# Two graph layers in one pass: layer 1's sums and blocks, q's writes, the flag and three loads put into other steps

## The chip, the core and the metric

The kernel runs on one core of a Trainium2 chip. The core has five engines that run their own instruction streams and wait for one another by semaphores: TensorE (PE in the profile; PEld is its weight load), VectorE (DVE), ScalarE (ACT), GpSimd (POOL) and SyncE (SP), which here only issues DMAs. Each engine runs its instructions in the order of the program, so one that waits holds back everything behind it on its engine; this is true of the DMAs that SP and POOL issue, too. The metric is the time of one execution on the device in microseconds.

## The reference, cut to what matters

Sixteen graphs of 1024 nodes with 256 features pass through two layers. Each layer normalises the nodes, applies relu and adds its result to its input.

```python
# layer 0: masked attention, 8 heads of 32 features
h = relu(layernorm(x))
Q, K, V = proj(h, Wq, bq), proj(h, Wk, bk), proj(h, Wv, bv)
scores = where(adj == 0, -inf, Q @ K.T * HD ** -0.5)
x = x + (softmax(scores) @ V) @ Wo.T + bo

# layer 1: attention by the kind of edge; each kind k has a vector a_k
h = relu(layernorm(x))
e_k = leaky_relu((h * a_k) @ h.T, 0.2)
scores = e_0 where adj == 1, e_1 where adj == 2, e_2 where adj == 3, e_3 where adj == 4, else -9e15
x = x + softmax(scores) @ h
```

In the inputs adj holds only 0 and 1. The kernel's main pass computes layer 1 with a_0 alone; a flag for each tile of adj records whether other kinds occur, and a second pass behind the main one, which these inputs skip, does such graphs again.

## The kernel before, in words

The unit of work is a tile of 128 rows (query nodes) of one graph; there are 16 x 8 = 128 of them. The program's order is written out by hand under `tc.manual_schedule()`: a loop over s = 0 to 136 (L720), called a round here, and in it a loop over the steps h = 0 to 7 (L723), one for each head. With b, t = divmod(s, 8), t = 0 is a graph's first round. In round s several tiles are at different stages:

- `now` is the tile of layer 0 whose heads are scored: per step two score matmuls of 512 columns (L415) into one of two PSUM tiles, the masked maximum on VectorE (L427), and a step later the exponential on ACT (L435). `was` is the tile of the round before and `gone` that of two rounds before; `nxt` is the tile that comes.
- `piece` and `piece_was` are a tile of nodes eight to nine rounds ahead of its use: normalised, turned, projected to k, v and q. The k and q halves are written to DRAM (L295, L301) and loaded again as keys (L336, on POOL, in steps of the last and first round of a graph) and queries (L382, on SP, step 1).
- `edge` is the tile of layer 1 scored in this round, nine rounds behind layer 0; `edge_was` is that of the round before, whose sums are made in this one.

The probabilities have to be turned before they are multiplied with the values. Heads 1, 3, 5, 7 are turned by eight TensorE transposes (L527) and two ACT copies (L528), two steps after their scores. Heads 0, 2, 4, 6 (`BY_BLOCKS`) and layer 1's tile are turned by VectorE within blocks of 32 (L356, `turn_blocks`) and moved to their places by four DMAs of 128 KB on SP's queue (L361, `placed`, called by `place_blocks`). Heads 0 to 5 are turned in steps 2 to 7 of their own round, heads 6 and 7 in steps 0 and 1 of the next. The sums over heads 0 to 3 (`combine(0)`, L470, 32 small matmuls, which are 64 rows of the trace; over key tiles, and within one over the four heads) come in step 7, those over heads 4 to 7 (`combine(1)`) in step 3 of the next round. Behind them in step 4 come the query projections of `piece_was` (L257), which write the bank `early` out of which VectorE takes v (`biased`, L331) at the start of that step, and the output projection (L485), for which VectorE makes oT (L480). In step 5 VectorE makes the layer's result x1 with its statistics (`residual`), POOL follows with some 18 small instructions that give scale and shift (`norm_of`, L143), and ACT normalises in step 7 (L506); TensorE transposes that at the end of step 0 (L513) and ACT copies it into layer 1's key table h1T (L517).

Layer 1's tile is scored in steps 0 and 1 (L549), its maximum and its leak are taken in steps 2 and 3 (L563, L571), its exponential in step 4 (L575), and its blocks are turned in step 5. Its sums (`gather`, L593) and `store` (L602, L603) come a round later. Its places, the tile pT1, exist once; so do adj, x1b, sel and ha. The mask of a tile (`mask`, L397, POOL) is kept for ten tiles, since layer 1 uses it again; `flag` (L406, ACT) squares adj less one half and sums the row.

On SP, one ordinary round issues, from step 0: k's first half (1), head 6 of `was` (4), k's second half (1), the next queries (1), head 0 (4), head 2 (4), q's two halves (2, step 6), head 4 (4, step 6), x1d (1), out (1, step 7), layer 1's blocks (4, step 7).

Of the kernel before, what the change touches and what calls it, by code (L numbers as in the profile page):

```python
# [42 lines left out]
def gnn_kernel(  # L43
# [131 lines left out]
    class Piece:  # L175
# [5 lines left out]
        def __init__(self, b, first, n=1):  # L181
            self.b, self.first, self.n = b, first, n
            self.cols = slice(first * P, (first + n) * P)
            self.projected, self.halved, self.again = [], [], []
            self.tags = ("xin", "h0", "hT", "halves", "hTm") if n == 1 else ("pT", "pT", "qt", "p", "blocks")

        def buffer(self, i, shape, dtype=F32):
# [88 lines left out]
        def split(self):  # L276
            which, oc, ps, bias, halves, parts = self.halved.pop(0)
            nc.vector.scalar_tensor_tensor(  # L278
                parts[:, 1], ps, bias[:, oc : oc + 1], parts[:, 0].bitcast(F32), ALU.add, ALU.subtract
            )  # L280
            halves = halves.bitcast(F32)
            if which == 0:
                self.write_keys(oc, halves, nc.sync, 0)
                if self.n > 1:
                    self.write_keys(oc, halves, nc.scalar, 1)
                self.again.append((oc, halves))
            elif self.n > 1:
                to = qds[self.b][self.first : self.first + self.n, oc]
                for twice in range(2):
                    (nc.sync, nc.scalar)[twice].dma_start(  # L290
                        out=to[:, :, twice].rearrange("t p w n -> p t (w n)"),
                        in_=halves.rearrange("p (t x) -> p t x", t=self.n),
                    )
            else:
                nc.sync.dma_start(  # L295
                    out=qds[self.b][self.first, oc].rearrange("p u w n -> p u (w n)"),
                    in_=halves.unsqueeze(1).to_broadcast([P, 2, 2 * P]),
                )
# [71 lines left out]
    class Attend:  # L370
# [21 lines left out]
            nc.gpsimd.dma_start(out=self.xb, in_=mixed(x[self.b, self.rows, :]))  # L392

        def mask(self):
            self.neg = work.tile([P, N], BF16, tag="neg", bufs=KEPT)
            masks[self.b, self.t] = self.neg
            nc.gpsimd.tensor_scalar(self.neg, self.adj, 0.0, MASKED, ALU.is_equal, ALU.mult)  # L397
            self.sums = small.tile([P, HEADS], F32, tag="sums")

# [2 lines left out]

        def flag(self):

            i = self.b * NT + self.t
            nc.scalar.activation(  # L406
                self.adj.bitcast(F32), self.adj, AF.Square, bias=less_half,
                accum_out=kinds_seen[:, i : i + 1],
            )

        def scores(self, h):
# [271 lines left out]
    with tc.manual_schedule():  # L683
# [8 lines left out]
        now, piece_next = attend_of(0), piece_of(0)  # L692
        nxt = attend_of(1)
        now.load()
        now.mask()
        now.flag()
        nxt.load()
        piece_next.load()
        for piece in first:
# [20 lines left out]
        for s in range(B * NT + LAG + 1):  # L720
            b, t = divmod(s, NT)
            nxt2, edge_nxt, piece_nxt = attend_of(s + 2), edges_of(s + 1), piece_of(s + 1)
            for h in range(HEADS):  # L723
                ending, eh = (now, h - 1) if h >= 1 else (was, HEADS - 1)
                turning, th = (now, h - 2) if h >= 2 else (was, HEADS + h - 2)


                if now:
                    now.scores(h)
                if h == 0 and piece_was:  # L730
                    piece_was.split()
                if h == 1 and piece_was:
                    piece_was.split()
                if h == 2 and edge:
                    edge.softmax_max()
                if h == 3 and edge:
                    edge.leak()
                if h == 4 and piece_was:
                    piece_was.biased()
                if h == 4 and was:  # L740
                    was.combined()
                if h == 5 and was:
                    was.residual()
                if h == 6 and piece_was:
                    piece_was.split()
                    piece_was.split()
                if h == 7 and edge_was:
                    edge_was.store()
                if now:
                    now.softmax_max(h)  # L750


                if ending:
                    ending.softmax_exp(eh)


                if turning and th in BY_BLOCKS:
                    turning.turn_blocks(th)
                    turning.place_blocks(th)
                elif turning:  # L760
                    turning.turn(th, 0)
                    turning.turn(th, 1)


                if h == 0:
                    if piece_was:
                        piece_was.write_again()
                    if edge:
                        edge.score(0)
                    if gone:  # L770
                        gone.turn_normed()
                        gone.turned_normed()
                    if nxt and s:
                        nxt.load()
                    if edge_was:
                        edge_was.load_nodes()
                if h == 1:
                    if edge:
                        edge.score(1)
                    if was:  # L780
                        was.reciprocals()
                    if piece:
                        piece.stats()
                        piece.scaled()
                    if piece_was:
                        piece_was.write_again()
                    if nxt:
                        nxt.load_queries()
                if h == 2:
                    if piece_was:  # L790
                        piece_was.values()
                    if was:
                        was.turn_reciprocals()
                        was.turned_reciprocals()
                        was.add_bias()
                if h == 3:
                    if was:
                        was.combine(1)
                    if nxt:
                        nxt.mask()  # L800
                if h == 4:
                    if piece_was:
                        piece_was.project(1, 0)
                        piece_was.project(1, 1)
                    if was:
                        was.output()
                    if piece:
                        piece.normed()
                    if edge:
                        edge.softmax_exp()  # L810
                    if edge_nxt:
                        edge_nxt.prepare()
                if h == 5:
                    if piece:
                        piece.turn()
                    if edge_was:
                        edge_was.gather(0)
                    if piece_was:
                        piece_was.high()
                        piece_was.high()  # L820
                    if piece:
                        piece.turned()
                    if piece_nxt:
                        piece_nxt.load()
                    if edge:
                        edge.turn_blocks()
                if h == 6:
                    if edge_was:
                        edge_was.gather(1)
                    if was:  # L830
                        was.keep()
                    if now:
                        now.load_nodes()
                    if nxt:
                        nxt.flag()
                    if piece:
                        piece.project(0, 0)
                        piece.project(0, 1)
                if h == 7:
                    if now:  # L840
                        now.combine(0)
                    if edge:
                        edge.place_blocks()
                    if piece:
                        piece.high()
                        piece.high()
                    if was:
                        was.normed()
                if now and t == NT - 1 and b + 1 < B and h in KEY_STEPS:
                    load_key(b + 1, KEY_STEPS.index(h))  # L850
                if now and t == 0 and b > 0 and HEADS + h in KEY_STEPS:
                    load_key(b, KEY_STEPS.index(HEADS + h))
            gone, was, now, nxt = was, now, nxt, nxt2
            edge_was, edge = edge, edge_nxt
            piece_was, piece = piece, piece_nxt
# [52 lines left out]
```

## Time and profile before

| | us |
|---|---|
| five runs, median | 3498.61 |
| lowest and highest of them | 3485.57 to 3503.91 |
| the profiled execution's own time | 3488.9 |
| its span, first to last instruction | 3487.1 |
| TensorE, VectorE, ACT, POOL busy in it | 3134.0, 2782.6, 2436.9, 2281.7 |
| mean granted TensorE clock | 0.969 of full speed |

The page of the profile gives busy time by engine, groups of instructions by line of the program with the idle time of their engine before them and what ended it ("<-"), and DMAs with the median time from issue to landing: 3.9 us for the blocks (2560 issues), 6.3 us for adj, 4.6 us for the queries, 5.8 us for the keys. A "wait" is idle time of an engine that another engine's instruction, or a DMA, ended; waits of an engine that is not the bottleneck cost nothing by themselves. In a timeline each row has its start, its length, the engine, the line, the operation and how many of them were merged ("x4"), and in brackets the idle time before it. SPq is SP's queue of instructions, and the length of a row there is that of issuing, not of moving the data.

### The profile page before, as it was taken

How to read it: one execution, taken by the hardware profiler on the slowest of the kernel's cores; microseconds unless marked ns; L12 is line 12 of the kernel's file. 1: busy time of each engine (PE TensorE's matmuls, PEld its weight loads, DVE VectorE, ACT ScalarE, POOL GpSimd, SP SyncE). 2: the span in 40 equal slices, each digit the busy share in tenths (PEclk: the TensorE clock that was granted, in tenths of full speed). 3: DMA queues.
4: the chain of work that ended last, by engine and by line, in shares of the span. 5: the costliest groups of instructions: out<-in, count | busy, mean ns of one | idle time of the engine just before them, and what ended most of it. 6: DMA issues, size and time to landing. Idle time of an engine off the chain costs nothing. (4 is left out here: it accounts for less than half of the span.)

```text
span 3487.1 us, 100532 instructions
## 1 busy us (share of the span) xinstructions
PE 3134.0 (90%) x36018; PEld 2278.1 (65%) x36018; DVE 2782.6 (80%) x5111; ACT 2436.9 (70%) x4829; POOL 2281.7 (65%) x6008
## 2 busy tenths in 40 slices
PE   5778999999999999999999999999999999998997
PEld 3666666666666666666676666666666666666653
DVE  3778878788788888888888788888878888887863
ACT  2777767677677777777777777777767777776750
POOL 2677667667667676667767767667667766765431
PEclk8999999999999999999999999999999999999999
DMA  5777787877778687786777778677787877777642
GB/s 211 207 220 225 211 250 209 246 220 222 229 224 247 202 240 226 209 256 206 246 221 219 244 216 244 204 229 235 207 248 217 248 212 213 243 219 231 189 131 76
DMA packets 747594, 763.10 MB, mean 219 GB/s; under 512 B 71792, under 2 KB 692592, under 8 KB 747088
## 3 DMA queue, kind: packets, MB, share of 16 engines
q1 hardware_dynamic: 678800, 542.21, 51.9%
q0 software_dynamic: 65088, 210.16, 20.0%
q8 instruction: 291, 4.77, 0.6%
q10 hardware_dynamic: 3200, 4.19, 0.3%
q14 instruction: 215, 1.76, 0.1%
HBM read 252.98 MB, written 167.77 MB: 121 GB/s over the span
## 5 line engine op out<-in xcount | busy, mean ns | idle before, releaser
L435 ACT ACTIVATE p<-p,nmx 128x1024 f32<-128x1024 f32 x1024 | 1185.9, 1158 | 414.4 <-DVE nmx L427 407.9
L427 DVE CUSTOM_DVE_ANT_0 p<-s,neg 128x1024 f32<-128x1024 f32 x1024 | 1243.0, 1214 | 205.2 <-PE s L415 204.2
L415 PE MATMUL s<-k,qt 128*128 128x512 f32 x2048 | 800.2, 472 | 34.5 <-DVE nmx L427 17.9
L470 PE MATMUL acc<-pT,v 128*32 128x128 f32 x16384 | 600.5, 289 | 238.5 <-DMA pT<-blocks 234.0
L470 PEld LDWEIGHTS acc<-pT,v 128*32 128x32 f32 x16384 | 494.6, 116 | 314.3 <-issue 216.6
L528 ACT COPY pT<-trp 128x512 f32<-128x512 f32 x1024 | 544.8, 584 | 132.2 <-PE trp L527 127.5
L356 DVE STREAM_TRANSPOSE blocks<-p 128x1024 f32<-128x1024 f32 x512 | 635.1, 1240 | 0.8 <-issue 0.8
L527 PE MATMUL trp<-ident,p 128*128 128x128 f32 x4096 | 533.3, 273 | 0.0
L527 PEld LDWEIGHTS trp<-ident,p 128*128 128x128 f32 x4096 | 481.6, 141 | 69.9 <-issue 1.2
L593 PE MATMUL acc<-h,pT 128*32 128x256 f32 x8192 | 510.8, 384 | 9.0 <-DMA pT<-blocks 8.2
L549 PE MATMUL s<-h1T,ha 128*128 128x512 f32 x1024 | 481.3, 593 | 0.5 <-ACT h1T L517 0.5
L397 POOL TENSOR_SCALAR neg<-adj 128x1024 bf16<-128x1024 int32 x128 | 467.7, 3654 | 18.6 <-DVE top L563 6.8
L415 PEld LDWEIGHTS s<-k,qt 128*128 128x128 f32 x2048 | 332.0, 193 | 217.9 <-issue 135.0
L593 PEld LDWEIGHTS acc<-h,pT 128*32 128x32 f32 x8192 | 246.7, 110 | 225.3 <-issue 79.7
L160 POOL TENSOR_SCALAR sq<-sq 128x1 f32<-128x1 f32 (+1 forms) x750 | 266.5, 355 | 65.5
L454 POOL COPY wide<-rec 128x256 f32<-128x256 f32 x128 | 51.2, 400 | 383.6 <-DVE rec L452 383.6
L301 POOL DMA_DIRECT2D kd<-halves x240 | 174.6, 727 | 165.6 <-DVE halves L278 148.7
L549 PEld LDWEIGHTS s<-h1T,ha 128*128 128x128 f32 x1024 | 183.9, 190 | 141.2 <-issue 128.7
L563 DVE CUSTOM_DVE_ANT_0 sel<-s,neg 128x1024 f32<-128x1024 f32 x128 | 156.7, 1224 | 70.9 <-PE s L549 70.9
L435 ACT ACTIVATION_READ_ACCUMULATOR p<-p,nmx 128x1 f32 x1024 | 202.6, 198 | 0.0
L517 ACT COPY h1T<-acc 128x256 f32<-128x256 f32 x128 | 47.7, 372 | 210.4 <-PE acc L513 210.4
L575 ACT ACTIVATE sel<-sel,nmx 128x1024 f32<-128x1024 f32 x128 | 145.3, 1135 | 64.5 <-DVE sel L571 64.5
(106 smaller groups left out, 4379.5 us busy)
## 6 DMA issues: line engine op xcount, KB each, us to landing
pT<-blocks SPq DMA_DIRECT2D x2560, 128.0 KB, 3.9
qt<-qd SPq DMA_DIRECT2D x128, 512.0 KB, 4.6
adj<-in_adj POOLq DMA_DIRECT2D x127, 512.0 KB, 6.3
qd<-halves SPq DMA_DIRECT2D x240, 256.0 KB, 2.6
k<-kd POOLq DMA_DIRECT2D x120, 512.0 KB, 5.8
kd<-halves SPq DMA_DIRECT2D x240, 128.0 KB, 4.2
kd<-halves POOLq DMA_DIRECT2D x240, 128.0 KB, 3.8
xb<-in_x POOLq DMA_DIRECT2D x128, 128.0 KB, 3.6
```

What stands on the lines that cost most here:

```text
L160: g.tensor_scalar(sq, sq, 1.5, None, ALU.add)
L301: queue.dma_start(out=kds[self.b][oc, :, :, twice, self.cols], in_=halves.rearrange("p (w n) -> p w n", w=2),)
L356: nc.vector.transpose(blocks.rearrange("p b j q -> p j b q"), p)
L397: nc.gpsimd.tensor_scalar(self.neg, self.adj, 0.0, MASKED, ALU.is_equal, ALU.mult)
L415: nc.tensor.matmul(self.ps[:, cols], lhsT=self.qt[:, h, :], rhs=keysets[self.b][h][:, cols], start=True, stop=True,)
L427: nc.vector.tensor_tensor_reduce(out=p, in0=sides[h in (3, 5, 7)], in1=self.neg, scale=-SCALE, scalar=FLOOR, op0=ALU.add, op1=ALU.min, acc ...
L435: nc.scalar.activation(p, p, AF.Exp, bias=nmx, scale=-1.0, accum_out=self.sums[:, h : h + 1])
L470: nc.tensor.matmul(sums_place[r * HD : (r + 1) * HD, g * P : (g + 1) * P], lhsT=vs[self.b][:, j, place_of(h) : place_of(h) + HD], rhs=self ...
L527: nc.tensor.transpose(tr[:, j, :], p[:, jj * P : (jj + 1) * P], ident)
L528: copy(pT[:, half * 4 : half * 4 + 4, :], tr)
L549: nc.tensor.matmul(self.e[:, cols], lhsT=self.ha[:, c, :], rhs=h1Ts[self.b][:, c, cols], start=(c == 0), stop=(c == NC - 1),)
L593: nc.tensor.matmul(sums_place[a * HD : (a + 1) * HD, :], lhsT=self.pT[:, j, a], rhs=h1s[self.b][:, j, :], start=(j == 0), stop=(j == NT - 1),)
```

## The change

The same instructions are issued, in other places:

- `gather(0)` and `gather(1)` of layer 1 go from steps 5 and 6 to steps 4 and 5, the first behind the output projection, the second behind the turn of `piece`.
- layer 1's `place_blocks` goes from step 7 to step 5, right behind its `turn_blocks`, and so ahead of head 4's blocks (step 6) on SP.
- q's two halves are no longer written to DRAM at the end of `split` (step 6, ahead of head 4's blocks) but by a new `write_queries` in step 7, behind `out`.
- `flag` goes from step 6 to step 3, ahead of `mask`, and writes its square into `neg`, which the mask then overwrites, in place of into adj itself. So the mask on POOL waits for ACT.
- adj is loaded in step 4 of the round before, behind the mask that reads the tile last, in place of step 0.
- layer 1's x1 is loaded in step 2 in place of step 0, on POOL, between `add_bias` and the mask.
- `turned_normed` (L517) goes from the end of step 0 to step 1, behind ACT's exponential of head 0.

The diff, cut to its core:

```diff
             else:
+                self.queries.append((oc, halves))
+
+        def write_queries(self):
+            for oc, halves in self.queries:
                 nc.sync.dma_start(
                     out=qds[self.b][self.first, oc].rearrange("p u w n -> p u (w n)"),
                     in_=halves.unsqueeze(1).to_broadcast([P, 2, 2 * P]),
...
         def mask(self):
+            nc.gpsimd.tensor_scalar(self.neg, self.adj, 0.0, MASKED, ALU.is_equal, ALU.mult)
+            self.sums = small.tile([P, HEADS], F32, tag="sums")
...
+        def flag(self):
...
+            i = self.b * NT + self.t
             self.neg = work.tile([P, N], BF16, tag="neg", bufs=KEPT)
             masks[self.b, self.t] = self.neg
...
             nc.scalar.activation(
-                self.adj.bitcast(F32), self.adj, AF.Square, bias=less_half,
-                accum_out=kinds_seen[:, i : i + 1],
+                self.neg, self.adj, AF.Square, bias=less_half, accum_out=kinds_seen[:, i : i + 1]
             )
...
                     ending.softmax_exp(eh)
 
+                if h == 1 and gone:
+                    gone.turned_normed()
...
                     if gone:
                         gone.turn_normed()
-                        gone.turned_normed()
-                    if nxt and s:
-                        nxt.load()
-                    if edge_was:
-                        edge_was.load_nodes()
                 if h == 1:
...
                         was.add_bias()
+                    if edge_was:
+                        edge_was.load_nodes()
                 if h == 3:
                     if was:
                         was.combine(1)
                     if nxt:
+                        nxt.flag()
                         nxt.mask()
                 if h == 4:
...
                         was.output()
+                    if edge_was:
+                        edge_was.gather(0)
...
                         edge_nxt.prepare()
+                    if nxt2:
+                        nxt2.load()
                 if h == 5:
                     if piece:
                         piece.turn()
                     if edge_was:
-                        edge_was.gather(0)
+                        edge_was.gather(1)
...
                         edge.turn_blocks()
+                        edge.place_blocks()
                 if h == 6:
-                    if edge_was:
-                        edge_was.gather(1)
                     if was:
                         was.keep()
                     if now:
                         now.load_nodes()
-                    if nxt:
-                        nxt.flag()
...
                 if h == 7:
                     if now:
                         now.combine(0)
-                    if edge:
-                        edge.place_blocks()
+                    if piece_was:
+                        piece_was.write_queries()
                     if piece:
                         piece.high()
                         piece.high()
```

More of the change, by code (lines that the diff above doesn't have):

```diff
@@ L183, in __init__ @@
             self.cols = slice(first * P, (first + n) * P)
-            self.projected, self.halved, self.again = [], [], []
+            self.projected, self.halved, self.again, self.queries = [], [], [], []
             self.tags = ("xin", "h0", "hT", "halves", "hTm") if n == 1 else ("pT", "pT", "qt", "p", "blocks")
@@ L394, in mask @@
         def mask(self):
-            self.neg = work.tile([P, N], BF16, tag="neg", bufs=KEPT)
-            masks[self.b, self.t] = self.neg
             nc.gpsimd.tensor_scalar(self.neg, self.adj, 0.0, MASKED, ALU.is_equal, ALU.mult)
@@ L405, in flag @@
             i = self.b * NT + self.t
+            self.neg = work.tile([P, N], BF16, tag="neg", bufs=KEPT)
+            masks[self.b, self.t] = self.neg
             nc.scalar.activation(
-                self.adj.bitcast(F32), self.adj, AF.Square, bias=less_half,
-                accum_out=kinds_seen[:, i : i + 1],
+                self.neg, self.adj, AF.Square, bias=less_half, accum_out=kinds_seen[:, i : i + 1]
             )
@@ L694, in gnn_kernel @@
         now.load()
+        now.flag()
         now.mask()
-        now.flag()
         nxt.load()
```

## The prediction, made before the changed kernel ran

> **What bounds the kernel now.** I read the shares by engine first, then the list of waits, then the timelines of one round (one pass of the loop over s, eight steps h) engine by engine. S is the start of a round's first score matmul; times "S + x" are us after it.
>
> ```profile
> PE 3134.0 (90%) x36018; PEld 2278.1 (65%) x36018; DVE 2782.6 (80%) x5111; ACT 2436.9 (70%) x4829; POOL 2281.7 (65%) x6008
> L470 PE MATMUL acc<-pT,v 128*32 128x128 f32 x16384 | 600.5, 289 | 238.5 <-DMA pT<-blocks 234.0
> ```
>
> TensorE is busy 90%, and of its 353 us of idle time 234 stand before one line: L470, the sums of layer 0, waiting for the DMAs that place a transposed head (pT<-blocks).
>
> ```profile
> PE acc L470 <- DMA pT<-blocks: 234.0, 122, 5.4
> ACT h1T L517 <- PE acc L513: 210.4, 122, 2.4
> POOL wide L454 <- DVE rec L452: 383.6, 127, 6.0
> DVE oT L480 <- PE acc L470: 103.3, 75, 5.6
> ```
>
> 122 waits in 128 rounds: one a round. L470 runs twice a round, combine(0) in step 7 and combine(1) in step 3; sorted by place, 233 us belong to combine(1), and its first four rows run (two matmuls, heads 4 and 5), so the missing tile is the next one: head 6, turned in step 0. One round (S = 1560.47), first the queue of SP:
>
> ```profile
> 1561.09 0.60 SPq L603 DMA_DIRECT2D out<-ot  x1
> 1561.79 3.67 SPq L361 DMA_DIRECT2D pT<-blocks  x4
> 1565.56 0.57 SPq L301 DMA_DIRECT2D kd<-halves  x1
> 1566.23 2.51 SPq L361 DMA_DIRECT2D pT<-blocks  x4
> ```
>
> ```profile
> 1562.51 1.24 DVE L356 STREAM_TRANSPOSE blocks<-p 128x1024 f32<-128x1024 f32 x1
> ...
> 1570.99 1.21 DVE L427 CUSTOM_DVE_ANT_0 p<-s,neg 128x1024 f32<-128x1024 f32 x1
> ...
> 1572.14 0.42 DVE L331 TENSOR_TENSOR v<-acc,bv_t 128x256 f32<-128x256 f32 x1
> ```
>
> ```profile
> 1569.06 0.41 PE L470 MATMUL acc<-pT,v 128*32 128x128 f32 x4
> 1571.05 1.94 PE L470 MATMUL acc<-pT,v 128*32 128x128 f32 x60 [1.58 <-DMA pT<-blocks]
> 1572.92 0.74 PE L415 MATMUL s<-k,qt 128*128 128x512 f32 x2
> 1573.50 1.05 PE L257 MATMUL acc<-hTm,wqT 128*128 128x128 f32 x8
> ```
>
> VectorE has head 6 turned at 1563.75, but SP issues its four DMAs only from 1566.23: the four of layer 1's tile (1561.79) and k's write stand ahead. Over rounds 17 to 117, for t = 1 to 7: head 6 is turned at S + 3.28, its DMAs are issued from S + 4.54, the last at S + 7.22, and TensorE resumes at S + 10.63, 3.41 us later; it was ready at S + 8.59. At t = 0, the first round of a graph: last issue S + 8.42, resume S + 14.35, ready S + 9.59.
>
> **What the bubble hides.** VectorE's last maximum before the sums ends at S + 11.74 in every ordinary round (11.72 at the least), then comes v (0.42 us), to S + 12.1. The query projections (L257, hTm) overwrite the bank that v reads, so they cannot start before about S + 12.15. They start at S + 13.36 on average for t = 1 to 7 and at S + 18.49 for t = 0; from there to the next S it is 12.2 us in both (periods 25.52 and 30.77). So of a 1.6 us bubble only 13.36 - 12.15 = 1.21 us can come back; the rest becomes a wait of L257 for v.
>
> **The parts.**
>
> *Layer 1's blocks issued in step 5 instead of step 7, its gathers a step earlier.* From the turn of head 4 to the last DMA of head 6, SP issues 4 + x1d + out + 4 + k + 4 = 15 now and, with q's two writes come in, 4 + x1d + out + 2 + k + 4 = 13 after. One costs 0.60 to 0.65 us. But the gathers (1.87 us each, the spacing from 1576.90 to 1578.77) now stand before the scores of heads 5 and 6, so these move back: laying the same durations end to end from L257 at S + 12.15 (0.89 projections, 0.68 output, 1.87 gather, 0.65 scores, 0.87 turn, 0.31 piece, 1.87 gather) puts the scores of head 6 at S + 19.3, and VectorE turns head 4 by S + 22.4, 1.9 us before the next S (S + 24.3) instead of 3.5 (now 1555.76 + 1.24, before 1560.47). The last issue for head 6 is then 12 issues of 0.65 after that: S + 5.95 if nothing holds the queue, 7.2 at worst (as now). With the 3.41 us from issue to resume: 9.4 to 10.6. A resume up to S + 9.55 costs nothing (1.9 for the sums, 0.6 for the scores, to 12.15). The added wait is on SP: the blocks of step 5 overwrite the tile that gather(1) reads, so they go out when it ends, S + 19.3 to 21.9; behind them stand only head 4's, not turned before S + 22.4. gather(0) overwrites the sums that oT is made from, but the output ahead of it waits for oT already. I take a projection start of S + 12.4: 0.96 us a round, between 0.2 and 1.21. Rounds with layer 1's tiles and t > 0: 105, so 101 us.
>
> *t = 0.* There head 6's DMAs take 5.93 us to resume, among key loads, adj (512 KB) and x1 (128 KB) issued in step 0; adj and x1 go elsewhere. Against it, the keys of heads 2 and 3 are issued on POOL after a chain that gets 1.4 us longer (below), and scores already wait there (L415 <- DMA k<-kd, 11.1 us in all). I take projections at S + 14.5, bounds 13.4 and 17: 4.0 us, 14 rounds, 56 us.
>
> *flag before mask* (ACT to step 3; POOL's mask now waits for it).
>
> ```profile
> 1570.05 1.05 ACT L528 COPY pT<-trp 128x512 f32<-128x512 f32 x2
> 1572.31 1.15 ACT L435 ACTIVATE p<-p,nmx 128x1024 f32<-128x1024 f32 x1 [1.21 <-DVE nmx L427]
> ```
>
> ```profile
> 1573.60 3.65 POOL L397 TENSOR_SCALAR neg<-adj 128x1024 bf16<-128x1024 int32 x1
> ...
> 1583.16 0.22 POOL L164 TENSOR_SCALAR shift<-shift 128x1 f32<-128x1 f32 x1
> ```
>
> ACT sits idle 1.21 us where the flag goes (1.17 + 0.2 us), so the next exponential slips by 0.2 us and ACT, busy 70%, absorbs it. The flag ends near S + 12.0; the mask starts at S + 11.7 on average now, and 0.68 us later with x1's load ahead of it. Wait: 0, at most 0.3 us. Writing bf16 in place of f32: nothing to gain or lose beyond a tenth of the 1.17 us, off the path.
>
> *x1 and adj loads* on POOL, 0.68 us each, go from step 0, where POOL idles 3.0 us a round for `wide` (383.6 / 127), into its dense stretch ahead of the normalisation: the last shift ends at S + 24.7 instead of 23.3. ACT is ready for it at S + 24.0, and head 7's exponential behind it (1.35 us) is needed by the turn at next S + 2.98; that leaves about 0.9 us unused. Cost 0, or up to 0.3 us a round with keys in the queue (t = 7). Both transfers are needed half a round or more later.
>
> *h1T's copy a step later on ACT* takes away 210 us of ACT idle, off the path; head 0's exponential comes earlier and nobody waits for it. 0. *q's writes in step 7* are counted in SP's 13; their readers come seven rounds on. The nine last rounds (layer 1 alone, 9.5 us each) issue the blocks before `out`: 0.5 us each, 5 us.
>
> **Sum:** 101 + 56 + 5 = 162 us from 3488.9, the profiled execution (span 3487.1): 3327. The five runs' median, 3498.61, is 9.7 above it: 3337.
>
> **Two rules weighed.** First the rows, around a bubble of 1.84 us:
>
> ```profile
> 1646.90:1648.80 1.90, 0.10 (x2) 0.00 (x0) 1.90 (x3) 1.73 (x4) 1.63 (x4) 1.00 0.73 210
> 1648.80:1652.40 3.60, 3.57 (x61) 3.21 (x61) 1.28 (x3) 2.56 (x4) 3.35 (x6) 0.53 0.90 277
> ```
>
> The granted clock falls to 0.53 behind it (the last columns are clock, DMA share, GB/s). The Trainium skill (TensorE: Matmul & The Clock Gate, HAM oscillation) puts the harm at idle gaps above some 3.4 us; by it only the bubbles at t = 0 would cost clock, and the ordinary rounds would give back somewhat less than I take. This row speaks against so high a limit; my measured starts hold the slow clock already. The skill (DMA: Bandwidth & Descriptors, Issuing engines are not separate DMA queues) also calls the issue time usually small beside the transfer. Here four issues take 2.5 us and the landing 3.4; by the rule, moving the queue's order would save nearly nothing, which is the first rival.
>
> **Rivals.** (1) *Head 6 lands as late as before* (17%): SP's 13 start 1.5 us later in the round, and q's 512 KB now run just ahead. For it: 0.76 mean DMA share, and 2.68 us for four issues that cost 1.95 unhindered. Then 0.2 x 105 + 2 x 14 = 49 us: 3450. (2) *VectorE becomes the bound* (10%): after the change it idles perhaps 2 us of 24.4; if the late scores 5 and 6 cost it 0.5 us a round more, 119 x 0.5 = 60 us go back: 3397. (3) *Slower, by POOL* (6%): the mask waits for the flag, POOL carries the delay into the shift and ACT into every exponential behind it. It eats the 0.9 us unused, then the gain of 1.3 a round; it decides from a wait of 2.2 us on, that is, a flag ending at S + 14.6. At 3 us: 0.8 x 119 = 95 us, 3594. Against it is ACT's idle time above. The forecast itself: 67%.
>
> **Numbers.** Best bounds: 1.21 x 105 + 5.1 x 14 + 10 = 208, so 3290; 10 us, the distance between the profiled run and the median, are added below: 3280. The upper end takes in rival 1: 3450. A measurement of this kernel can tell about 0.3%, 10 us. Faster 0.90 (the forecast, rival 2 and 13 of rival 1's 17), within 0.04 (the other 4: a bubble that only changes its cause), slower 0.06 (rival 3).
>
> **What would show it.** Right: the wait of L470 for pT<-blocks falls from 234 us to under 80; a new wait of the query projections for v, some tenths to 1 us a round; last issue for head 6 near S + 6; periods near 24.5 and 26.5. Wrong: L470 still waits at S + 10 (rival 1); idle DVE before scores of heads 5 and 6 of over 2 us (rival 2); POOL's mask waiting for ACT by microseconds (rival 3).

## The result, and the profile after

| | before | after |
|---|---|---|
| median of all runs, us | 3498.61 (59 runs) | 3498.09 (33 runs) |
| profiled execution's span, us | 3487.1 | 3492.1 |
| mean granted TensorE clock | 0.969 | 0.987 |

The ratio after / before is 0.9999 [0.999, 1.0008]: no difference. I had forecast 3337. (Lines of the changed kernel's code stand four further down than before's from the projections on: L470 is L474, L602 is L606; L257 and L278 stay; flag is L411 and mask L399.)

First the shares by engine and the group of L474 (once L470), from the page of after:

```profile
PE 3130.3 (90%) x36018; PEld 2237.8 (64%) x36018; DVE 2795.7 (80%) x5111; ACT 2441.6 (70%) x4829; POOL 2266.2 (65%) x6008
L474 PE MATMUL acc<-pT,v 128*32 128x128 f32 x16384 | 565.2, 279 | 142.6 <-DVE ot L606 92.5
```

The busy times are those of before within 0.7%, except 1.8% less on PEld. In the group the idle time fell from 238.5 to 142.6 us, and, above all, **its releaser is another**: it was the DMA pT<-blocks, it is now VectorE's store of layer 1's output (ot, L606). The list of waits of after says it in full (engine, what waits, what ended it: total us, times, longest):

```profile
POOL wide L458 <- DVE rec L456: 527.1, 127, 12.3
...
DVE p L431 <- PE s L419: 394.8, 397, 4.6
...
PE acc L474 <- DVE ot L606: 92.5, 108, 1.7
...
PE acc L257 <- DVE v L335: 63.8, 86, 0.9
PE acc L474 <- DMA pT<-blocks: 48.3, 39, 3.2
...
POOL neg L399 <- ACT neg L411: 45.6, 12, 5.7
PE s L419 <- DMA k<-kd: 42.2, 28, 5.2
```

The wait for pT<-blocks went from 234.0 us to 48.3, and the new wait of the projections for v (63.8) is there, both as forecast. But once in each of some 108 rounds TensorE now stands before L474 for the store. The same waits in the list of before:

```profile
DVE p L427 <- PE s L415: 204.2, 345, 2.9
...
PE acc L470 <- DVE ot L602: 1.9, 6, 0.3
```

So the pair was in the list before the change, 1.9 us in six waits. All six lie in the last rounds, s = 120 to 126; in ordinary rounds the store still had 1.0 us to spare (table below). VectorE's waiting for scores has nearly doubled (204 to 395 us).

One ordinary round of after (S = 1584.03, next S = 1609.49), from the timeline of TensorE:

```profile
1596.18 1.16 PE L257 MATMUL acc<-hTm,wqT 128*128 128x128 f32 x8 [0.95 <-DVE v L335]
...
1605.58 1.03 PE L531 MATMUL trp<-ident,p 128*128 128x128 f32 x8
1607.40 2.16 PE L474 MATMUL acc<-pT,v 128*32 128x128 f32 x64 [0.79 <-DVE ot L606]
1609.49 0.73 PE L419 MATMUL s<-k,qt 128*128 128x512 f32 x2
```

and from that of VectorE in the same round:

```profile
1600.77 1.23 DVE L431 CUSTOM_DVE_ANT_0 p<-s,neg 128x1024 f32<-128x1024 f32 x1 [1.03 <-PE s L419]
...
1604.39 1.23 DVE L431 CUSTOM_DVE_ANT_0 p<-s,neg 128x1024 f32<-128x1024 f32 x1 [0.40 <-PE s L419]
...
1605.54 1.24 DVE L360 STREAM_TRANSPOSE blocks<-p 128x1024 f32<-128x1024 f32 x1
...
1606.86 0.48 DVE L606 SCALAR_TENSOR_TENSOR ot<-acc,rec,x 128x256 f32<-128x256 f32 x1
```

The projections start at S + 12.15 behind v: the bubble of `combine(1)` is gone. At the other end of the round TensorE is through with the transposes at 1606.6 and could go on, but `combine(0)` (1607.40) writes `sums_place` (L475), out of which the store (L606) reads until 1607.34. The store comes behind head 4's turn (1605.54), which comes behind the maxima of heads 5 and 6 (1600.77 and 1604.39), and these had to wait 1.03 and 0.40 us for scores that now stand behind the gathers.

The mean places in a round (t = 2 to 6, us after S) show that this is no single case:

| | before | after |
|---|---|---|
| last issue of head 6's blocks (t = 1 to 7) | 7.22 | 6.00 |
| `combine(1)` ends | 12.90 | 10.85 |
| query projections (L257) start | 13.45 | 12.15 |
| scores of head 5 | 15.04 | 15.97 |
| scores of head 6 | 18.74 | 19.58 |
| head 4 turned on VectorE | 22.09 | 22.74 |
| store ends on VectorE | 22.71 | 23.30 |
| TensorE through with the transposes of head 5 | 23.76 | 22.57 |
| `combine(0)` starts | 23.69 | 23.36 |
| next S | 25.6 | 25.45 |

TensorE gains 1.30 us by the projections and has 1.19 of it left when the transposes are done (23.76 against 22.57). Before, the store ended 1.0 us ahead of `combine(0)`; now TensorE waits for it, and 0.15 us of gain is left at the next S. The loss is in the row of L474 above: 0.79 us of waiting, and 2.16 us for the sums, which take 1.96 where they do not wait (the weights wait for ot as well, PEld 118.9 us in 111 waits). Together 1.0 us.

By sorts of rounds the span's change of +5.0 us is: 98 ordinary rounds with t > 0 (25.53 to 25.48 us) -5; 13 rounds with t = 0 (30.76 to 31.37) +8; the round s = 8 +5.9; s = 120 +1.5; the six rounds after it (23.03 to 24.34) +7.9; the last rounds -8.4; the start and the first rounds -5.

### The profile page after: what moved, and what is told of

Same layout as the page of the kernel before. It is cut to its first block, busy times and chain, and to the rows that moved or that the text cites. A ratio compares the mean times of both kernels' runs of the same rounds, so it can differ in the third digit from the quotient of the medians.

```text
span 3492.1 us, 100281 instructions
## 1 busy us (share of the span) xinstructions
PE 3130.3 (90%) x36018; PEld 2237.8 (64%) x36018; DVE 2795.7 (80%) x5111; ACT 2441.6 (70%) x4829; POOL 2266.2 (65%) x6008
## 3 DMA queue, kind: packets, MB, share of 16 engines
q14 instruction: 214, 1.75, 0.2%
## 5 line engine op out<-in xcount | busy, mean ns | idle before, releaser
L419 PE MATMUL s<-k,qt 128*128 128x512 f32 x2048 | 781.7, 464 | 69.4 <-DMA k<-kd 42.2
L474 PE MATMUL acc<-pT,v 128*32 128x128 f32 x16384 | 565.2, 279 | 142.6 <-DVE ot L606 92.5
L474 PEld LDWEIGHTS acc<-pT,v 128*32 128x32 f32 x16384 | 475.0, 112 | 214.7 <-DVE ot L606 118.9
L419 PEld LDWEIGHTS s<-k,qt 128*128 128x128 f32 x2048 | 319.7, 191 | 293.2 <-issue 186.7
L399 POOL TENSOR_SCALAR neg<-adj 128x1024 bf16<-128x1024 int32 x128 | 467.0, 3649 | 54.7 <-ACT neg L411 45.6
L160 POOL TENSOR_SCALAR sq<-sq 128x1 f32<-128x1 f32 (+1 forms) x750 | 240.8, 321 | 65.5
L567 DVE CUSTOM_DVE_ANT_0 sel<-s,neg 128x1024 f32<-128x1024 f32 x128 | 156.8, 1225 | 73.4 <-PE s L553 73.4
L161 POOL TENSOR_TENSOR r<-r,sq 128x1 f32<-128x1 f32 (+1 forms) x750 | 157.6, 210 | 62.5
L257 PE MATMUL acc<-hTm,wqT 128*128 128x128 f32 x960 | 138.3, 287 | 64.4 <-DVE v L335 63.8
```

The source lines that it names most:

```text
L160: g.tensor_scalar(sq, sq, 1.5, None, ALU.add)
L419: nc.tensor.matmul(self.ps[:, cols], lhsT=self.qt[:, h, :], rhs=keysets[self.b][h][:, cols], start=True, stop=True,)
L474: nc.tensor.matmul(sums_place[r * HD : (r + 1) * HD, g * P : (g + 1) * P], lhsT=vs[self.b][:, j, place_of(h) : place_of(h) + HD], rhs=self ...
```

## The experiments

Two theories. **A**: `combine(0)` waits for the store, and this wait alone holds the ordinary round; without it the gain forecast comes. **B**: the wait only stands where TensorE would otherwise wait for something else (VectorE with the late scores, a queue); without it the time stays. Each edit is against the changed kernel unless told otherwise, and each ratio against before, with runs of before on the same chip.

### Store and gather in the other quarter (e1_other_bank)

```diff
-    sums_place[a * HD : (a + 1) * HD, :], lhsT=self.pT[:, j, a], ...
+    brief[a * HD : (a + 1) * HD, :], lhsT=self.pT[:, j, a], ...
...
-    nc.vector.scalar_tensor_tensor(ot, sums_place, rec, self.x1, ALU.mult, ALU.add)
+    nc.vector.scalar_tensor_tensor(ot, brief, rec, self.x1, ALU.mult, ALU.add)
```

> The changed kernel with layer 1's sums in the quarter bank `brief` (free from step 3 on) in place of `sums_place`, so that combine(0) no longer has to wait until store has read them. Theory A (the bubble of combine(1) is gone, and what it left was eaten by combine(0) waiting for store, which VectorE reaches late because the scores of heads 5 and 6 moved back): combine(0) starts at S + 22.6 instead of 23.4 to 24, periods fall from 25.45 to 24.5 us, and the nine last rounds by some 1.4 each: 119 x 0.9 + 10 = 117 us less, about 3380. Theory B (VectorE's whole chain through a round is the bound, and the wait for store is only where it shows): the wait moves to another line, within 10 us of 3498.

3498.92 us, 1.0005 [0.9985, 1.0025]. In the list of waits of this kernel:

```profile
PE acc L474 <- DVE ot L606: 94.0, 108, 1.7
```

The wait did not go (92.5 us in the changed kernel, 108 times in both), so this tells nothing on what the time would be without it. `sums_place` and `brief` are two halves of one tile, `banks[0]` (L89, L90); taking the store to the other half leaves the wait of the sums for it as it was. Inconclusive, and not for B: my edit missed its aim.

### The same edit on the kernel before (e4_before_other_bank)

> The kernel before with layer 1's sums in `brief` alone. Theory A: there the wait of combine(0) for store is only 1.9 us in all, so 3498 within 10. Theory C (the shared bank cost the kernel before as well, in some way the waits do not name): 50 us or more less.

3495.6 us, 0.9993 [0.9968, 1.0018]. The change of place by itself is worth nothing.

### The store a step earlier (e5_store_early)

```diff
-                if h == 7 and edge_was:
+                if h == 6 and edge_was:
                     edge_was.store()
```

On VectorE the store now stands ahead of head 6's maximum and head 4's turn, where VectorE was idle for scores; all other places are those of the changed kernel.

> The changed kernel with layer 1's store on VectorE in step 6, behind q's halves and ahead of head 6's maximum, in place of step 7. In the first experiment combine(0) waited for store at the same instants as before although its sums lay in another quarter: the two quarters share one PSUM tile, and the wait did not go. Here store is over before combine(0) comes up. Theory A: store ends near S + 20.6, head 6's maximum slips by some 0.2 us, combine(0) starts at S + 22.6, periods of 24.5 to 24.7 against 25.45, some 95 us less: 3400. Theory B (VectorE's chain through the round is the bound wherever store stands): the wait moves to another line and the time stays within 10 us of 3498.

3405.36 us, 0.9743 [0.9703, 0.9783]. The waits of this kernel:

```profile
DVE p L431 <- PE s L419: 195.3, 303, 4.3
...
PE acc L474 <- DMA pT<-blocks: 125.7, 106, 4.1
```

The wait for ot is gone, `combine(0)` starts at S + 22.77 in place of 23.36, the ordinary round (t > 0) takes 24.65 us in place of 25.48. **This decides for A**: one line, 2.6%. VectorE's waits fall back to 195 us though the scores of heads 5 and 6 lie later still (S + 16.24 and 19.86). In an ordinary round 1.13 us of that fall is the wait for head 0's scores (1.53 to 0.40), since S comes earlier, and 0.40 the wait for head 6's, which the store now fills; the wait for head 5's stays (1.01 to 0.95). Not all comes back, since head 4's turn is now behind the store and ends at S + 23.17; its four DMAs and all behind them on SP leave later, head 6's last at S + 6.98, and 0.8 us of the old bubble returns (125.7 us).

### Gathers back in steps 5 and 6 (e2_gathers_back)

```diff
+                if h == 6 and edge_was:
+                    edge_was.gather(1)
+                if h == 6 and edge:
+                    edge.place_blocks()
...
                 if h == 4:
-                    if edge_was:
-                        edge_was.gather(0)
...
                 if h == 5:
-                        edge_was.gather(1)
+                        edge_was.gather(0)
...
-                        edge.place_blocks()
```

The blocks overwrite what gather(1) reads, so they go with it into step 6, ahead of head 4's.

> The changed kernel with the gathers back in steps 5 and 6; layer 1's blocks are issued in step 6, ahead of head 4's. Theory A: the scores of heads 5 and 6 come early again, VectorE reaches store in time and combine(0) does not wait; head 6's last DMA is issued near S + 6.4 and TensorE resumes by S + 9.9, projections start at S + 12.4, period 24.6: about 100 us less, 3400. Theory B: within 10 us of 3498.

3424.86 us, 0.979 [0.9754, 0.9827]. The waits of this kernel:

```profile
PE acc L474 <- DMA pT<-blocks: 133.5, 108, 4.9
...
PE acc L474 <- DVE ot L606: 0.5, 1, 0.5
```

With the scores of heads 5 and 6 ahead again the wait for ot is all but gone, `combine(0)` starts at S + 22.88, and rounds with t > 0 take 24.80 us. Head 6's last issue falls back to S + 7.03, and with it some of the old bubble returns, which leaves the time 25 us above theory A's 3400. A second way to take the new wait away, with the same outcome: A.

### Layer 1's blocks back in step 7 (e3_blocks_back)

```diff
                 if h == 5:
-                        edge.place_blocks()
...
                 if h == 7:
+                    if edge:
+                        edge.place_blocks()
```

> The changed kernel with only layer 1's place_blocks back in step 7, behind combine(0). Theory A: the bubble of combine(1) comes back (resume near S + 10.6, 1.2 us later projections) and the wait for store stays, so both are paid: period 26.6, 105 x 1.2 = 126 us more, about 3620. If the order on SP's queue was never worth anything (my prediction's first rival): 3498.

3718.34 us, 1.0647 [1.0605, 1.0688], slower than expected. From this kernel's waits:

```profile
PE acc L474 <- DMA pT<-blocks: 309.3, 122, 9.3
...
PE acc L474 <- DVE ot L606: 96.5, 111, 1.7
```

Both waits, one after the other, in each round of 27.3 us. Head 6's last issue goes from S + 6.00 to 8.53 and TensorE resumes at S + 11.33 in place of 8.82; the landing stays at 2.80 us (2.82 in after). So the order on SP moves the resumption one for one, and it is worth 220 us in this kernel. Rival 1 of the prediction, that the order was worth nothing, falls.

### adj and x1 loaded in step 0 again (e6_loads_back), adj alone (e12_adj_back)

```diff
                 if h == 0:
+                    if nxt and s:
+                        nxt.load()
+                    if edge_was:
+                        edge_was.load_nodes()
...
                 if h == 2:
-                    if edge_was:
-                        edge_was.load_nodes()
                 if h == 4:
-                    if nxt2:
-                        nxt2.load()
```

> The changed kernel with adj and x1 loaded in step 0 again; the flag stays in step 3 ahead of the mask. Ordinary rounds stay at 25.45, since combine(0)'s wait for store sets them. In the first round of a graph (31.5 us) the keys of heads 2 and 7 are then issued some 1.3 us earlier and without adj just ahead: their waits (42 us in all) fall to some 11, while head 6's DMAs land later again (adj among them). Net 1 to 2 us in each of 15 rounds: 3475 to 3490. If the loads' place has no part in it: 3498.

3632.28 us, 1.0387 [1.0353, 1.0421]: a miss, since I had costed this part only for the round t = 0. From this kernel's page and its waits:

```profile
L474 PE MATMUL acc<-pT,v 128*32 128x128 f32 x16384 | 621.0, 289 | 358.4 <-DMA pT<-blocks 255.7
```

```profile
PE acc L474 <- DMA pT<-blocks: 255.7, 121, 5.8
...
PE acc L474 <- DVE ot L606: 102.2, 118, 1.7
```

The bubble is back in every round, by another way than in e3: head 6's last issue is at S + 6.58 (0.6 later), but its landing takes 4.23 us in place of 2.82. Moving adj alone,

```diff
                 if h == 0:
+                    if nxt and s:
+                        nxt.load()
```

(with its line of step 4 taken out) was to show which load it is.

> The changed kernel with only adj loaded in step 0 again (x1 stays in step 2). With both loads in step 0 it took 3632, since head 6 then landed 4.23 us after its last issue instead of 2.82. If the packets of adj (512 KB) are what slows head 6, nearly all of that stays: 3590 to 3630, landing 3.9 to 4.2. If POOL's queue or x1 does it: below 3550.

3589.11 us, 1.0233 [1.0209, 1.0257]: landing 3.83 us, last issue S + 6.63, resume S + 10.47, and 214.7 us for pT<-blocks. That speaks for adj's packets, though time and landing both end just under what I had put for them. Of the 1.65 us by which TensorE resumes later than in after, 1.01 is the landing and 0.63 the later last issue. By the ratios, each taken on its own chip, adj alone (512 KB) costs some 82 us of e6's 135, and x1 (128 KB) by difference the other 54; x1 alone was not tried. The Trainium skill (DMA: Bandwidth & Descriptors, Issuing engines are not separate DMA queues) says that transfers started by different engines run on the same DMA engines and interleave; POOL's adj beside SP's blocks, 2.82 us against 3.83, agrees with that. The next sentence of it calls the time of issuing usually small beside the transfer; e3, where four issues were moved and the last issue for head 6 came 2.5 us later, does not bear that out here.

### The two ways out with the loads in step 0 (e7_store_early_loads_back, e8_gathers_loads_back)

The edits of e5 and of e6 together, and those of e2 and of e6.

> The two edits before together. Theory A: both gains, 3400 less 10 to 20, about 3385; head 6 lands somewhat later with adj in step 0, but has 0.7 us to spare in ordinary rounds (resume S + 8.8 against 9.55). Theory B: as the loads alone.

> The kernel with the gathers back in steps 5 and 6 (3425) and adj and x1 loaded in step 0 as well. First rounds of a graph fall from 32.2 to about 30.5 (15 x 1.7 = 25 us), but head 6, which resumes at S + 9.95 there, lands later among adj's packets, by up to 0.3 us in 105 rounds (30 us): 3400 to 3430.

3688.22 us, 1.0529 [1.048, 1.0579], and 3686.89, 1.0548 [1.0504, 1.0592]: misses for the same reason, and worse than e6. In e7 head 4 is turned 1.5 us before the next S in place of 2.7, since the store stands ahead of it, and SP is later with it. In e8 it is turned 3.5 us before the next S, but its blocks stand behind layer 1's, which wait for `gather(1)` and go out only from 4.2 us before the next S (5.7 in e6): last issue for head 6 at S + 8.17, landing 3.54, resume 11.71.

The longer bubbles cost clock as well. TensorE waits 358.0 and 345.6 us for pT<-blocks; behind 99 and 88 of these waits (35 in e6) the rest of the sums runs slow, up to 3.63 us for 60 rows that otherwise take 1.94, and the mean granted clock is 0.936 and 0.943, against 0.971 in e6. So the store's earlier place, worth 93 us with the loads moved, costs 56 us with them in step 0.

### Keys earlier, q later, both (e9_keys_early, e10_queries_later, e11_keys_and_queries)

These start from e5 and go for what was left: the keys that layer 0 waits for at t = 0, and q's 512 KB on SP behind `out`.

```diff
-    KEY_STEPS = (2, 3, 5, 6, 8, 9, 11, 12)
+    KEY_STEPS = (1, 2, 3, 4, 5, 6, 10, 11)
```

> The kernel with store in step 6 (3405), and the keys of the next graph loaded in steps 1 to 6 of a graph's last round and 2, 3 of its first, in place of 2, 3, 5, 6 and 0, 1, 3, 4. It touches only these two rounds of eight. If the first round (31.2 us against 24.6) is long because 512 KB key loads are issued just as head 6's DMAs run and because keys 2 and 7 come late, it falls by 2 to 4 us, 15 times: 3345 to 3375; the last round may pay up to 1 us for POOL's longer chain. If it is long for another reason: 3405.

3403.05 us, 0.9709 [0.9688, 0.973]: about e5's time, and not the gain that I had forecast. Scores wait for keys 1.0 us in all (38.3 in e5), but rounds with t = 0 still take 30.9 us: there SP issues head 6's last DMA only at S + 10.0. In e10 the keys stay and q's writes go from step 7 to step 2 of the next round:

```diff
                 if h == 2:
+                    if piece_gone:
+                        piece_gone.write_queries()
...
                 if h == 7:
-                    if piece_was:
-                        piece_was.write_queries()
...
-            piece_was, piece = piece, piece_nxt
+            piece_gone, piece_was, piece = piece_was, piece, piece_nxt
```

> The kernel with store in step 6 (3405), and q's two writes put into step 2 of the next round, out of SP's queue ahead of head 6. Last issue for head 6 at S + 5.7 instead of 6.98, resume near S + 8.7 instead of 9.83, which is below the 9.55 that v allows: projections from 12.49 to 12.15, 0.35 us in 105 rounds, 37 us less: 3370. If head 6 is late for its packets and not for the queue: 3405.

3400.01 us, 0.97 [0.9677, 0.9723]: 30 us above the forecast, though head 6 was late for the queue. Here the ordinary round is what the prediction had laid out: last issue S + 5.87, projections 12.19, `combine(0)` 22.54, period 24.4 us (t = 3 to 6) against the S + 24.3 of my sum. But scores wait 74.4 us for keys, and rounds with t = 0 take 31.7 (31.2 in e5).

> Both edits on the kernel with store in step 6: the sum of their gains, 3310 to 3340.

Both edits: 3355.08 us, 0.9566 [0.9546, 0.9586], the best version and faster than both kernels, 15 us above the range forecast. Alone the two edits took 0.3% and 0.4% off e5's ratio, together 1.8%. From its page:

```profile
L474 PE MATMUL acc<-pT,v 128*32 128x128 f32 x16384 | 544.5, 279 | 63.6 <-DMA pT<-blocks 61.2
```

Rounds with t = 0 fall to 28.5 us, which neither edit did alone: SP's queue held them in the one, late keys in the other. Rounds with t > 0 take 24.6. It is 18 us above what I had forecast for the changed kernel, with three more edits (the store, the keys, q).

## Why the prediction was wrong, point by point

- **The bubble and its cause: right.** Head 6's blocks were late by SP's order. Last issue forecast S + 5.95, measured 6.00; e3 confirms that the order did it.
- **The floor by v: right.** "They cannot start before about S + 12.15": 12.15 is the measured mean, with a wait for v of 63.8 us. I took 12.4 for the projections, so this part came out slightly better than forecast.
- **The failed step: "laying the same durations end to end from L257 at S + 12.15 ... VectorE turns head 4 by S + 22.4, 1.9 us before the next S (S + 24.3)".** The durations were right to 0.3 us (head 6's scores at S + 19.58 against 19.3; e10's round takes 24.4), but they were laid for TensorE alone. By my own numbers the sums before that next S begin at 24.3 - 1.96 = S + 22.3, while the store stands behind the turn on VectorE and ends 0.6 us after it (22.09 and 22.71 before): 22.4 + 0.6, so S + 23.0. It reads what those sums overwrite. I weighed one overwriting of `sums_place` (gather(0) over what oT reads) and not the other. Measured: head 4 turned at 22.74, store to 23.30, sums at 23.36. That gives back 1.0 us in an ordinary round (the wait stands 108 times in the list); of the 0.96 us that I took for an ordinary round, 0.05 is left. e5 and e2 show it by two edits.
- **Rival 2 (VectorE, 0.5 us a round): the right place, the wrong mechanism and size.** VectorE does come late because of the scores of heads 5 and 6, but no work of VectorE bounds the round, one store does. My sign for it, "idle DVE before scores of heads 5 and 6 of over 2 us", was too high: 1.43 us in the round shown did it.
- **t = 0: the wrong sign.** Forecast -4.0 us each, measured +0.61. Three rows of the changed kernel's round at S = 1501.55:

```profile
1508.68 0.70 PE L419 MATMUL s<-k,qt 128*128 128x512 f32 x2 [1.39 <-DVE top L567]
...
1514.97 3.37 PE L474 MATMUL acc<-pT,v 128*32 128x128 f32 x60 [2.63 <-DMA pT<-blocks]
...
1529.51 0.73 PE L419 MATMUL s<-k,qt 128*128 128x512 f32 x2 [1.50 <-DMA k<-kd]
```

  The sums still wait 2.63 us for head 6: over such rounds its last issue is at S + 6.75 (8.42 before), but the landing takes 6.85 us, where I had hoped for less than the 5.93 of before with adj and x1 gone. The first row is head 2's scores and the last head 7's, and both wait for their keys: in the first the list names VectorE's L567, which reads the other score tile, but the key of head 2 landed at 1508.54, 0.14 us ahead of the row. Over such rounds TensorE waits 1.35 us before head 2 and 1.25 before head 7. So for keys, which I bounded only by a row of 11.1 us, TensorE waits 42.2 us by the list, and more by waits named like the first. e9 to e11 show SP's queue and the keys each holding these rounds. What holds the last 4 us (28.5 against 24.6) was not tried.
- **The loads' place: the term was too small.** I put the loads of adj and x1 at 0 outside t = 0. e6 shows 134 us: without that move the bubble would not have gone (TensorE resumes at S + 10.81 there, 10.63 before). That the bubble went as forecast hangs on a part that the forecast gave no credit, and in this it was lucky.
- **flag before mask: right.** POOL waits 45.6 us for it, but in 12 waits, eight of them in rounds 119 to 126, not one a round; rival 3 is out. **The nine last rounds:** forecast -5, measured -8.4 for the last stretch. The +7.9 of the six rounds before it I had not foreseen: it is the same wait for the store, 1.7 us in each (0.1 to 0.3 before), and without it, in e5, they take 22.4 to 22.9 us. Nor the +5.9 of s = 8: there the scores of head 6 wait 5.17 us for their key (0.43 before).
- **Open:** whether the sums wait for the store because the two lie in one bank or because the wait is set for the whole tile `banks[0]`: e1 showed only that the other half does not help. A store from the other tile, which has its own readers in those steps, was not tried.

## What to carry to other kernels

When a stall on one engine goes, write down for every buffer that this engine overwrites afterwards when its last reader on another engine is done, and compare the two with the new times: the next bound can be a pair that today stands in the list of waits with almost nothing (here 1.9 us in six waits, none of them in an ordinary round). If matrix work is pulled ahead of scores, the engine that lives on these scores gets later while TensorE gets earlier, so slack between them shrinks from both sides (1.0 us before, -0.8 after). And undo single parts of a change that "did nothing": taken back, one of its parts cost 220 us, another 134, and a third gained 73 (e3, e6, e2).

## What was not expected of the hardware

A landing depends on what other queues move at the same time: the four DMAs of 128 KB of one head took 2.82 us from the last issue to TensorE's resumption without adj and x1 in those steps, 3.83 with adj's 512 KB, 4.23 with adj's and x1's. By the DMA's own rows the last of the four landed 2.70, 3.71 and 4.10 us after its issue.

The granted clock is not what it seems to be worth. Two stretches around a wait of after, the first the end of the t = 0 bubble of 2.63 us, the second around the 0.79 us before `combine(0)` (after the length: busy us of PE, PEld, VectorE, ACT, POOL, then clock, DMA share, GB/s):

```profile
1515.00:1519.00 4.00, 4.00 (x63) 3.44 (x63) 0.56 (x2) 2.02 (x5) 3.92 (x2) 0.63 1.03 322
...
1608.00:1612.00 4.00, 4.00 (x64) 2.71 (x54) 2.47 (x6) 2.37 (x6) 1.90 (x3) 1.00 0.89 276
```

After 2.63 us of idle time TensorE had 0.63 of its clock for the next stretch; after 0.79 us it had all of it; the prediction's row had 0.53 after 1.84 us. The length of a wait alone does not decide it. Over all runs' traces, the 60 rows behind a wait inside `combine(1)` took 1.94 us after every one of 617 waits of 0.25 to 1.75 us; they were slower, up to 3.63 us, after 295 of 543 waits of 1.75 to 3.5 us, and after all 113 longer ones. What decides in between no run here shows.

The round of after shown above has two gaps, 0.95 and 0.79 us, in place of one, and the clock is 1.00 over the whole of it; over the execution the mean rose from 0.969 to 0.987. It brought nothing, because the ordinary round now hangs on VectorE's store and not on TensorE's speed. A higher clock in the profile is no sign of a shorter time; a lower one can be part of a longer one (e7, e8).

Rounds that hang on the chain TensorE, VectorE, TensorE are strikingly regular: in the changed kernel the periods for t = 3 to 5 scatter by 0.01 to 0.02 us (standard deviation), where before, when they hung on DMAs, the same rounds scattered by 0.9 to 1.3.
